# Two experts with small remainders share one block of rows

## The chip, the cores and the metric

The kernel runs on one core of a Trainium2 chip. The time is the device time of one launch in microseconds (us). The kernel before took 860.69 us in the median of three runs (860.58 to 861.32). A core has five engines with instruction queues of their own: TensorE (PE: products, into the PSUM memory), VectorE (DVE), ScalarE (ACT), GpSimd (POOL) and SyncE (SP, here a queue for transfers). Each works through its own queue in order and waits on semaphores for the others. Transfers run on 16 DMA engines; a transfer belongs to the queue of the engine that issues it.

## The reference

Two decoder layers, each of attention, cross-attention and a feed-forward part, run over x of 4 x 256 tokens with 256 features. All parts but the last are the same in both kernels. The last one is a mixture of experts: each token chooses 6 of 28 experts, and their outputs are summed with the softmax weights of the choice.

```python
logits = x @ gate_weight.T
scores = softmax(logits)
topk_w, topk_idx = top_k(scores, 6)
topk_w = topk_w / (topk_w.sum(-1) + 1e-20)
cw = zeros((T, E)).at[arange(T)[:, None], topk_idx].add(topk_w)
for wg, wu, wd, w_tok in zip(w_gate, w_up, w_down, cw.T):   # 28 experts
    h = silu(x @ wg) * (x @ wu)                               # 256 -> 176
    y = y + w_tok[:, None] * (h @ wd)                         # 176 -> 256
```

Here T is 1024, so there are 6144 pairs of a token and an expert. On the reference's inputs an expert gets between 117 and 302 tokens.

## The kernel before

**Lists and blocks.** `_route` writes, for each of the four batches, every token's row (its 256 features, its number as an integer, the weights of all its experts; 288 values) into DRAM, once for each chosen expert: into `lists`, where every expert has room for 1024 rows. `lists` is filled beforehand with blank rows, whose numbers point to spare rows behind the result (1024 to 1151). The work is then cut into *blocks*: 128 rows of one expert. When an expert's number of tokens is not a multiple of 128, its last block is filled up with blank rows.

Twelve blocks (`EARLY`) that are full after five of the eight token tiles start early, while the last batch is still being routed. `_blocks` counts the tokens of each expert, subtracts the early blocks, takes the running sum over experts by a product with a triangular matrix, and `_tables` makes three tables of NBLK entries from it: the expert of each block (packed in words for TensorE's registers), the row of `lists` at which it starts (for SP's registers), and the expert's number on every partition. The code runs `USUAL` = 50 late blocks without a condition, and the rest, up to NBLK, under `tc.If`. On these inputs there are 50 late blocks.

**One block.** `load` fetches 128 rows (xb; the pool has EARLY + 2 = 14 buffers). `turned` transposes them on TensorE (tpx) and copies them out on ScalarE (Tx). `gate_up` multiplies by the expert's gate and up weights, which lie in SBUF for all experts at once and are addressed by a register (pgu, 352 columns, two steps over the features), then SiLU on ScalarE (sg) and a product on VectorE (eh). `hidden` transposes eh and copies it out on VectorE (Th). `down` multiplies by the down weights (py, two steps of 88), picks the row's weight for this expert on VectorE (wjunk, wsel), scales on ScalarE (ys; NACC + 2 = 5 buffers), and GpSimd adds the 128 rows into an accumulator in DRAM by an indirect transfer, at the token numbers that xb carries (L998). A float32 product appears in the trace as two matmul records, so a block has four for pgu and four for py.

**The order.** In `rest`, step j issues the load of block j + 4, then gate_up(j), down(j - 1), turned(j + 2) and hidden(j). A scheduler then sets each engine's final order. In `early`, down is put off by LAG = 8 steps, because the down weights arrive late.

**The accumulators.** There are NACC + NLATE = 5 arrays. Their adds go round in turn; two adds into the same array wait for each other. From block LATE = 16 on, only the last two arrays are used, and in the meantime the other three are read back and added to x: `sums` loads a pair of token tiles (part; 6 buffers), and VectorE adds them (L1085), spread over the steps by `join_sums`. When all blocks are done, the last two arrays are read back in eight loads on the queues of SP and ACT (L1072), added (L1103), and the output is written (L1104).

Of the kernel before, what the change touches and what calls it, by code (L numbers as in the profile page):

```python
# [11 lines left out]
F32 = mybir.dt.float32  # L12
I32 = mybir.dt.int32
BF16 = mybir.dt.bfloat16
AF = mybir.ActivationFunctionType
ALU = mybir.AluOpType
# [4 lines left out]
P = 128  # L21
B, S, C = 4, 256, 256
# [11 lines left out]
E, M, TOPK = 28, 176, 6  # L34
MH = M // 2
# [1 line left out]

EARLY, FULL = 12, 5
SURE = min(EARLY, (FULL * P * TOPK - E * (P - 1) + P - 1) // P)
NBLK = (B * S * TOPK + E * (P - 1)) // P - SURE  # L40
TRASH = E * B * S
ROW = 288
NACC = 3
USUAL = 50
NLATE, LATE = 2, USUAL - 34


K_ID, K_MASK, K_TRI, K_ONES = 0, 128, 256, 384
# [2 lines left out]
K_BLK = K_BASE + E  # L51
K_STEP = K_BLK + NBLK
K_OF = K_STEP + B * S // P
# [823 lines left out]
def _blocks(nc, tc, env):  # L877

    psum, cst, ones, tri, rt1, seen, done = (env[n] for n in ("psum", "cst", "ones", "tri", "rt1", "seen", "done"))
    pn = psum.tile([P, 8], F32, tag="tp", name="pn")  # L880
    nc.tensor.matmul(pn[:E, 0:1], seen[:, NT], ones[:, 0:1], start=True, stop=True)
    cnt = rt1.tile([E, 1], F32, name="cnt")
    nc.vector.tensor_copy(cnt, pn[:E, 0:1])
    nb = rt1.tile([E, 1], F32, name="nb")
    junk = rt1.tile([E, B * S // P], F32, name="bjunk")
    nc.vector.tensor_scalar(junk, cst[:E, K_STEP:K_OF], cnt, None, ALU.is_lt, ALU.add, accum_out=nb)
    nc.vector.tensor_tensor(nb, nb, done, ALU.subtract)
    yield
    pc = psum.tile([P, 8], F32, tag="tp", name="pcum")
    nc.tensor.matmul(pc[:E, 0:1], tri[:E, :E], nb, start=True, stop=True)  # L890
    nc.tensor.matmul(pc[:E, 1:2], ones[:E, :E], nb, start=True, stop=True)
    first = rt1.tile([E, 2], F32, name="first")
    nc.vector.tensor_copy(first, pc[:E, 0:2])
    total = rt1.tile([1, 1], I32, name="total")
    nc.vector.tensor_copy(total, first[0:1, 1:2])
    off = rt1.tile([E, 1], F32, name="off")
    nc.vector.tensor_tensor(off, cst[:E, K_OF : K_OF + 1], done, ALU.add)
    nc.vector.tensor_tensor(off, off, first[:, 0:1], ALU.subtract)
    env["rest"], _ = yield from _tables(nc, env, "1", NBLK, first[:, 0:1], nb, off)
    env["total"] = total  # L900


class _Blocks:


    AHEAD = 4
    LAG = 8

    def __init__(self, ctx, nc, tc, env):
        self.nc, self.tc, self.psum, self.cst, self.ident = (nc, tc, env["psum"], env["cst"], env["ident"])  # L910
# [4 lines left out]
    def begin(self, ctx, wdn):  # L915
        self.wdn = wdn
        self.ek = ctx.enter_context(self.tc.tile_pool(name="ek", bufs=2))

    def values(self, table, engine, top, j, n):
        _, vals = self.nc.values_load_multi_w_load_instructions(  # L920
            table[:, j : j + n],
            [engine],
            min_val=0,
            max_val=top,
            skip_runtime_bounds_check_because="the table's entries are clamped to these bounds",
        )
        return vals

    def words(self, table, n):

        nc = self.nc
        loaded = self.values(table, mybir.EngineType.PE, (1 << 20) - 1, 0, (n + 3) // 4)

        def expert(i):
            e = nc.tensor.snap((loaded[i // 4] >> (5 * (i % 4))) & 31)
            return nc.s_assert_within(
                e, 0, E - 1, skip_runtime_bounds_check_because="the table's entries are clamped to these bounds"
            )

        return expert  # L940

    def load(self, row, queue):
        xb = self.eb.tile([P, ROW], F32, tag="xb", name="xb")
        queue.dma_start(xb, self.lists[bass.ds(row, P), :])
        return xb
# [9 lines left out]
    def gate_up(self, xT, e):  # L955
        nc = self.nc
        g = self.psum.tile([P, 2, 512], F32, tag="sc", name="pgu")
        pg = g[:, 0, : 2 * M]
        for k in range(2):
            nc.tensor.matmul(  # L960
                pg, xT[:, k, :], self.wgu[:, bass.ds(e * (4 * M) + k * 2 * M, 2 * M)], start=(k == 0), stop=(k == 1)
            )
        sg = self.ek.tile([P, M], F32, tag="sg", name="sg")
        nc.scalar.activation(sg, pg[:, :M], AF.Silu)  # L964
        h = self.ek.tile([P, M], F32, tag="h", name="eh")
        nc.vector.tensor_tensor(h, pg[:, M:], sg, ALU.mult)  # L966
        return h, g[:MH, 1, : 2 * P].rearrange("p (k n) -> p k n", k=2)

    def hidden(self, h, tp):
        for k in range(2):  # L970
            self.nc.tensor.transpose(tp[:, k, :], h[:, k * MH : (k + 1) * MH], self.ident)  # L971
        hT = self.ek.tile([MH, 2, P], F32, tag="Th", name="Th", bufs=self.LAG + 2)
        self.nc.vector.tensor_copy(hT, tp)  # L973
        return hT

    def down(self, hT, e, xb, e_col, accs):
        nc = self.nc
        wsel = self.ek.tile([P, 1], F32, tag="wsel", name="wsel")
        junk = self.ek.tile([P, E], F32, tag="wjunk", name="wjunk")
        done = nc.vector.scalar_tensor_tensor(  # L980
            junk,
            self.cst[:, K_IOTA : K_IOTA + E],
            e_col,
            xb[:, C + 1 : C + 1 + E],
            ALU.is_equal,
            ALU.mult,
            accum_out=wsel,
        )
        if not self.puts:
            _stay_behind(self.tc, done, self.route["placed"])  # L990
        py = self.psum.tile([P, C], F32, tag="o", name="py")
        for k in range(2):
            nc.tensor.matmul(  # L993
                py, hT[:, k, :], self.wdn[:, bass.ds(e * (2 * C) + k * C, C)], start=(k == 0), stop=(k == 1)
            )
        y = self.ek.tile([P, C], F32, tag="ys", name="ys", bufs=NACC + 2)
        nc.scalar.activation(y, py, AF.Copy, scale=wsel)  # L997
        nc.gpsimd.indirect_dma_start(  # L998
            out=accs[self.puts % len(accs)],
            out_offset=bass.IndirectOffsetOnAxis(ap=xb[:, C : C + 1].bitcast(I32), axis=0),  # L1000
            in_=y,
            in_offset=None,
            compute_op=ALU.add,
        )
        self.puts += 1

    def load_early(self, rows):
        at = self.values(rows, mybir.EngineType.Pool, TRASH, 0, EARLY)
# [2 lines left out]
    def early(self, engine, words, rows, e_all):  # L1011
# [3 lines left out]
        es, hTs, before = [], [], None  # L1015
        for j in range(EARLY + self.LAG):
            if j < EARLY:
# [5 lines left out]
            if j + 2 < EARLY:  # L1023
                xTs.append(self.turned(xbs[j + 2]))
            if j >= self.LAG:
                n = j - self.LAG
                self.down(hTs[n], es[n], xbs[n], e_all[:, n : n + 1], self.acc)
            yield

    def rest(self, words, list_row, e_all):  # L1030
        nc = self.nc
        expert = self.words(words, NBLK)
        at, xbs = {}, {}

        def load(j, end):
            if j not in at:
                n = min(5, end - j)
                at.update(zip(range(j, j + n), self.values(list_row, mybir.EngineType.SP, TRASH, j, n)))
            xbs[j] = self.load(at.pop(j), nc.sync)

        def run(first, end, also=None):
            for j in range(first, min(first + self.AHEAD, end)):
                load(j, end)
            xTs = {j: self.turned(xbs[j]) for j in range(first, first + 2)}
            before = None
            for j in range(first, end):
                if j + self.AHEAD < end:
                    load(j + self.AHEAD, end)
                e = expert(j)
                h = self.gate_up(xTs.pop(j), e)  # L1050
                if before is not None:
                    self.down(*before)
                if j + 2 < end:
                    xTs[j + 2] = self.turned(xbs[j + 2])
                accs = self.acc if j < LATE else self.acc[NACC:]
                before = (self.hidden(*h), e, xbs.pop(j), e_all[:, j : j + 1], accs)
                if also is not None:
                    also(j)
            self.down(*before)

        return run


def _experts(ctx, nc, tc, x, out, env):

    acc = env["acc"]
    ep = ctx.enter_context(tc.tile_pool(name="ep", bufs=6))


    def sums(n, q, queue):  # L1070
# [7 lines left out]
    def join_sums(j):  # L1078
# [4 lines left out]
        if 0 <= j - LATE - 10 < len(adds):  # L1083
            n, t = adds[j - LATE - 10]
            nc.vector.tensor_tensor(x[t], x[t], parts[n, t // 2][:, t % 2, :], ALU.add)  # L1085

    run = env["blocks"].rest(*env["rest"])
    more = nc.values_load(
        env["total"], min_val=0, max_val=NBLK, skip_runtime_bounds_check_because="a sum of rounded counts, at most NBLK"
    )  # L1090
    run(0, USUAL, join_sums)
    with tc.If(more > USUAL):
        run(USUAL, NBLK)

    oview = out.rearrange("b (t p) c -> (b t) p c", p=P)
    queues = (nc.sync, nc.scalar)
    for q in range(NT // 2):
        late = [sums(NACC + n, q, queues[n]) for n in range(NLATE)]
        for i in range(2):
            t = 2 * q + i  # L1100
            engine = nc.gpsimd if t % 3 == 2 else nc.vector
# [791 lines left out]
def _constants():  # L1893
# [8 lines left out]
    c[:, K_BASE:K_BLK] = np.arange(E) * B * S + 1  # L1902
    c[:, K_BLK:K_STEP] = np.arange(NBLK)
    c[:, K_STEP:K_OF] = np.arange(B * S // P) * P
# [107 lines left out]
```

## Time and profile before

| | us |
|---|---|
| median of three runs | 860.69 |
| the profiled execution | 860.22 |
| its span, first to last instruction | 858.6 |
| first product of the late blocks | 702.3 |
| end of the last product | 839.9 |
| tail, last product to the end of the span | 18.7 |
| TensorE busy, 702.3 to 840.0 | 131.9 of 137.7 |
| VectorE, ScalarE, GpSimd busy in the same stretch | 54.1, 52.0, 81.9 |
| mean granted TensorE clock, whole span | 0.883 of full speed |

A line of the timeline gives the start, the length, the engine, the line of the kernel, the operation with output and inputs, and in brackets the idle time of the engine just before and what ended it. A line of the chain gives start, length, engine, tile and line; a step of the chain is cut where the next one begins. A line of the groups by form gives, after the count, the busy time in us and the mean of one in ns, then idle time before them. A line of the waits gives who waited for whom, the total in us, how often, and the longest. Ends of matmuls are modelled, so the distance from start to start is the better measure of them.

### The profile page before, as it was taken

The numbers are of one execution on the slowest core, as the hardware profiler recorded it, in microseconds if no ns is written. First come the engines' busy times: TensorE is split into PE (matmuls) and PEld (weight loads), VectorE is DVE, ScalarE is ACT, GpSimd is POOL, SyncE is SP. The second block draws the span as 40 slices with busy tenths as digits, with TensorE's granted clock in tenths as the row PEclk, the third lists the DMA queues.
The fourth block names the chain that finished last, engine by engine and source line by source line (L and its number), as shares of the span: only waits on it lengthen the run. The fifth ranks groups of instructions, "written<-read, shape, count | busy, mean of one in ns | idle before, by whom it ended". The sixth has DMA issues, their size and how long they took to land. (4 is left out here: it accounts for less than half of the span.)

```text
span 858.6 us, 12259 instructions
## 1 busy us (share of the span) xinstructions
PE 700.7 (82%) x3902; PEld 458.1 (53%) x3902; DVE 526.0 (61%) x1306; ACT 304.7 (35%) x992; POOL 324.6 (38%) x280
## 2 busy tenths in 40 slices
PE   8988998588988887979568646897888789889991
PEld 4546555355555564566325325565545457667770
DVE  4677567886563699885538996756545223353332
ACT  2255444342441401221046424455323134334430
POOL 3332122214220373430144530124455376546563
PEclk9999999789999796988788876999768699989996
DMA  8999999500505200141500000571137577767646
GB/s 302 281 337 324 326 326 331 204 1 0 185 19 214 77 2 0 46 151 50 165 1 1 0 1 1 213 300 63 63 114 200 188 128 119 149 173 112 104 56 167
DMA packets 84452, 117.94 MB, mean 137 GB/s; under 512 B 5822, under 2 KB 71487, under 8 KB 83874
## 3 DMA queue, kind: packets, MB, share of 16 engines
q1 hardware_dynamic: 70914, 98.56, 35.0%
q0 software_dynamic: 11808, 16.98, 11.2%
q10 hardware_dynamic: 1664, 1.57, 0.5%
q8 instruction: 35, 0.57, 0.3%
q14 instruction: 31, 0.25, 0.1%
HBM read 59.67 MB, written 55.33 MB: 134 GB/s over the span
## 5 line engine op out<-in xcount | busy, mean ns | idle before, releaser
L998 POOL DMA_INDIRECT acc<-ys,xb x62 | 97.7, 1576 | 71.2 <-ACT Tx L952 43.4
L960 PE MATMUL pgu<-wgu_e,Tx 128*128 x248 | 93.7, 504 | 5.5 <-ACT Tx L952 3.3
L417 POOL TENSOR_TENSOR pr<-pr,rs 128x512 f32<-128x512 f32 x32 | 41.9, 1312 | 131.8 <-DVE rs L415 69.1
L407 ACT ACTIVATE pr<-sc,nb 128x256 f32<-128x256 f32 x128 | 58.9, 474 | 49.8 <-DVE nb L402 49.6
L993 PE MATMUL py<-wdn_e,Th 88*128 x248 | 65.4, 391 | 4.7 <-DVE Th L973 2.8
L1749 ACT ACTIVATE xpr<-xsc,cnm 128x256 f32<-128x256 f32 (+1 forms) x128 | 52.1, 421 | 39.7 <-DVE cnm L1744 28.4
L797 POOL DMA_INDIRECT lists<-R,rows x48 | 47.0, 979 | 37.4 <-DVE rows L784 13.6
L960 PEld LDWEIGHTS pgu<-wgu_e,Tx 128*128 128x128 f32 x248 | 46.0, 205 | 24.5 <-issue 7.1
L993 PEld LDWEIGHTS py<-wdn_e,Th 88*128 88x128 f32 x248 | 47.4, 195 | 21.2 <-DVE Th L973 3.9
L1557 POOL TENSOR_TENSOR qk<-qkv 128x1024 f32<-128x1024 f32 x16 | 39.9, 2524 | 35.8 <-ACT qkv L1528 35.8
L107 PE MATMUL av<-pT,ckt 128*64 128x256 f32 x256 | 39.8, 409 | 15.4 <-DVE pT L433 10.5
L966 DVE TENSOR_TENSOR eh<-pgu,sg 128x176 f32<-128x176 f32 x62 | 21.0, 339 | 48.3 <-issue 26.0
L964 ACT ACTIVATE sg<-pgu 128x176 f32<-128x176 f32 x62 | 19.7, 317 | 76.3 <-PE pgu L960 64.5
L997 ACT ACTIVATE ys<-py,wsel 128x256 f32<-128x256 f32 x62 | 29.3, 473 | 44.5 <-PE py L993 35.8
L107 PE MATMUL xsc<-kz,xqT 64*128 64x128 f32 (+1 forms) x256 | 37.7, 397 | 7.5 <-ACT xpr L1749 6.5
L110 PE MATMUL x_tp<-cst,xpr 128*128 128x128 f32 x192 | 34.3, 309 | 10.4 <-ACT xrT L1792 3.3
L398 DVE TENSOR_REDUCE nm<-sc 128x4 f32<-128x1024 f32 x32 | 39.0, 1217 | 4.9 <-PE sc L107 4.5
L980 DVE SCALAR_TENSOR_TENSOR wjunk<-cst,e_all,xb 128x28 f32<-128x28 f32 x62 | 15.3, 247 | 42.7 <-ACT ys L997 41.9
L1549 POOL TENSOR_TENSOR qk<-qkv 128x1024 f32<-128x1024 f32 x16 | 35.6, 2254 | 14.2 <-ACT qkv L1521 8.6
L1611 DVE TENSOR_TENSOR pv<-s,qkv 128x2048 f32<-128x2048 f32 x16 | 40.6, 2538 | 0.1
L110 PE MATMUL tp<-cst,pr 128*128 128x128 f32 x256 | 38.1, 291 | 2.4 <-DVE pT L433 1.5
L1576 PE MATMUL as<-qk,cst 128*128 128x128 f32 x256 | 34.6, 298 | 6.1 <-POOL qk L1549 6.1
(377 smaller groups left out, 1569.7 us busy)
## 6 DMA issues: line engine op xcount, KB each, us to landing
lists<-blank SPq DMA_DIRECT2D x9, 3600.0 KB
wgu_e<-in_e_gu_dram SPq DMA_DIRECT2D x4, 2464.0 KB
xb<-lists SPq DMA_DIRECT2D x50, 144.0 KB
acc<-blank SPq DMA_DIRECT2D x5, 1152.0 KB
wdn_e<-in_e_dn_dram SPq DMA_DIRECT2D x4, 1232.0 KB
wq<-in_m_wq_dram SPq DMA_DIRECT2D x4, 1024.0 KB
mwo<-in_m_wo_dram SPq DMA_DIRECT2D x2, 2048.0 KB
part<-acc SPq DMA_DIRECT2D x16, 256.0 KB
```

The costliest lines, as they stand in the source:

```text
L107: self._next(self.engine.matmul(*args, **kw))
L110: self._next(self.engine.transpose(*args, **kw))
L398: nc.vector.tensor_reduce(nm, sc, AX.X, ALU.max, negate=True)
L407: nc.scalar.activation(pr[:, e, qt, :], sc[:, e, qt, :], AF.Exp, bias=nb[:, e, qt : qt + 1], accum_out=ss[:, e, qt : qt + 1],)
L417: nc.gpsimd.tensor_tensor(pr[:, 1], pr[:, 1], rs[:, 1].unsqueeze(2).to_broadcast([P, 2, S]), ALU.mult)
L797: done = nc.gpsimd.indirect_dma_start(out=lists, out_offset=bass.IndirectOffsetOnAxis(ap=rows[:, i, n : n + 1], axis=0), in_=R[:, i, :], i ...
L960: nc.tensor.matmul(pg, xT[:, k, :], self.wgu[:, bass.ds(e * (4 * M) + k * 2 * M, 2 * M)], start=(k == 0), stop=(k == 1))
L993: nc.tensor.matmul(py, hT[:, k, :], self.wdn[:, bass.ds(e * (2 * C) + k * C, C)], start=(k == 0), stop=(k == 1))
L998: nc.gpsimd.indirect_dma_start(out=accs[self.puts % len(accs)], out_offset=bass.IndirectOffsetOnAxis(ap=xb[:, C : C + 1].bitcast(I32), axi ...
L1557: nc.gpsimd.tensor_tensor(pr[:, 4 * i : 4 * i + 4], q3[:, h0 : h0 + 4].unsqueeze(2).to_broadcast([P, 4, H, D]), k3.unsqueeze(1).to_broadca ...
L1611: nc.vector.tensor_tensor(pv, s[:, hh].unsqueeze(2).to_broadcast([P, 8, D, H]), v3.unsqueeze(1).to_broadcast([P, 8, D, H]), ALU.mult,)
L1749: nc.scalar.activation(pr[:, j, cols], sc[:, j, cols], AF.Exp, bias=nm[:, i, j : j + 1], accum_out=ss[:, i, h : h + 1])
```

## The change

An expert's remainder of at most 64 tokens no longer gets a block of its own. `_blocks` now counts two kinds: blocks that are full or have more than 64 tokens, and small remainders. Both get tables, by two calls of `_tables`. Two small remainders share one block, each in one half of the rows: a *pair*.

- For a pair, `copied` copies the gate, up and down weights of both experts on ScalarE from where they lie (addressed by a register on ScalarE) to fixed tiles gu and dn, one buffer each.
- `halves` gives, for a pair, the products of either half of the rows: 64 rows of the block against that half's copied weights, into the 64 partitions of that half in PSUM. So pgu and py have twice as many products in a pair, each with half the output rows.
- The load of a pair is two transfers of 64 rows.
- `down` sends a pair's y out twice, so that tokens which chose both experts are not added twice in one transfer: once with the first half at its token numbers and the second half at spare rows (`aside`), once the other way round, into two accumulators in turn. Four small copies on VectorE (both) make the two columns of numbers.
- `rest` now runs 37 blocks (`USUAL`) and 7 pairs (`UPAIR`), mixed so that every sixth item is a pair. More of either kind runs under `tc.If`.
- LATE becomes 37 + 7 - 34 = 10, counted in items. LAG becomes 5 for 8, and the pool of `part` has 3 buffers for 6.

```diff
-USUAL = 50
-NLATE, LATE = 2, USUAL - 34
+USUAL, UPAIR = 37, 7
+NLATE, LATE = 2, USUAL + UPAIR - 34
...
+    big = rt1.tile([E, 1], F32, name="big")
+    nc.vector.tensor_scalar(junk, cst[:E, K_STEP:K_OF], cnt, None, ALU.is_lt, ALU.add, accum_out=big)
+    nc.vector.tensor_tensor(nb[:, 0:1], big, done, ALU.subtract)
+    nc.vector.tensor_tensor(nb[:, 1:2], every, big, ALU.subtract)
...
+    bigs, _ = yield from _tables(nc, env, "1", NBLK, first[:, 0:1], nb[:, 0:1], off[:, 0:1])
+    (words, rows, e_all), _ = yield from _tables(nc, env, "2", E, first[:, 1:2], nb[:, 1:2], off[:, 1:2])
...
-    LAG = 8
+    LAG = 5
...
+    def halves(self, e):
+        if not isinstance(e, tuple):
...
+        return [
+            (
+                slice(i * HALF, (i + 1) * HALF),
+                lambda k, i=i: e[0][:, i, k * 2 * M : (k + 1) * 2 * M],
+                lambda k, i=i: e[1][:, i, k * C : (k + 1) * C],
+            )
+            for i in range(2)
+        ]
+    def copied(self, experts):
+        nc = self.nc
+        gu = self.ew.tile([P, 2, 4 * M], F32, tag="gu2", name="gu2")
+        dn = self.ew.tile([MH, 2, 2 * C], F32, tag="dn2", name="dn2")
+        for i, e in enumerate(experts):
+            nc.scalar.copy(gu[:, i], self.wgu[:, bass.ds(e * (4 * M), 4 * M)])
+            nc.scalar.copy(dn[:, i], self.wdn[:, bass.ds(e * (2 * C), 2 * C)])
+        return gu, dn
...
         for k in range(2):
-            nc.tensor.matmul(
-                pg, xT[:, k, :], self.wgu[:, bass.ds(e * (4 * M) + k * 2 * M, 2 * M)], start=(k == 0), stop=(k == 1)
-            )
+            for rows, gu, _ in self.halves(e):
+                nc.tensor.matmul(pg[rows], xT[:, k, rows], gu(k), start=(k == 0), stop=(k == 1))
...
         for k in range(2):
-            nc.tensor.matmul(
-                py, hT[:, k, :], self.wdn[:, bass.ds(e * (2 * C) + k * C, C)], start=(k == 0), stop=(k == 1)
-            )
+            for rows, _, dn in self.halves(e):
+                nc.tensor.matmul(py[rows], hT[:, k, rows], dn(k), start=(k == 0), stop=(k == 1))
...
+        places = [xb[:, C : C + 1].bitcast(I32)]
+        if isinstance(e, tuple):
+            both = self.ek.tile([P, 2], I32, tag="both", name="both")
+            for i in range(2):
+                for n in range(2):
+                    half = slice(n * HALF, (n + 1) * HALF)
+                    nc.vector.tensor_copy(both[half, i : i + 1], (places[0] if i == n else self.aside)[half])
+            places = [both[:, i : i + 1] for i in range(2)]
+        for place in places:
+            nc.gpsimd.indirect_dma_start(
+                out=accs[self.puts % len(accs)],
+                out_offset=bass.IndirectOffsetOnAxis(ap=place, axis=0),
...
+            self.puts += 1
...
+            for i in range(2):
+                nc.sync.dma_start(
+                    xb[i * HALF : (i + 1) * HALF], self.lists[bass.ds(row(kind, 2 * j + i, 2 * end), HALF), :]
+                )
+            copies[j] = self.copied([experts[1](2 * j + i) for i in range(2)])
...
+            items = [(0, j, b) for j in range(a, b)]
+            for j in range(c, d):
+                items.insert((j - c + 1) * ((b - a) // (d - c) + 1) - 1, (1, j, d))
...
-    ep = ctx.enter_context(tc.tile_pool(name="ep", bufs=6))
+    ep = ctx.enter_context(tc.tile_pool(name="ep", bufs=3))
...
-    run(0, USUAL, join_sums)
-    with tc.If(more > USUAL):
-        run(USUAL, NBLK)
+    run(((0, USUAL), (0, UPAIR)), join_sums)
+    with tc.If(more > 0):
+        run(((USUAL, NBLK), (UPAIR, E // 2)))
```

## The prediction

> **What bounds the kernel now.** I read the chain of waits first. From 702.3 us to 839.9 us the kernel runs its 50 late expert blocks, and the chain there stays on TensorE:
>
> ```profile
> 805.64 1.22 PE pgu L960 x4
> 806.86 0.86 PE py L993 x4
> 807.73 0.22 PE tpx L950 x2
> 807.95 0.22 PE pgu L971 x2
> 808.16 1.22 PE pgu L960 x4
> ```
>
> One block is four steps of TensorE, and the next starts 808.16 - 805.64 = 2.52 us later; over other blocks the mean is 2.53. 50 x 2.53 = 126.5 of the stage's 137.6 us; the rest is filling and a stall of 9 us near 746 to 766 us, where VectorE's adds of partial sums (L1085) wait for their loads and block the copies queued behind them (the waits, from 700 us to the end):
>
> ```profile
> DVE x_in L1103 <- DMA part<-acc: 11.2, 2, 9.8
> DVE x_in L1085 <- DMA part<-acc: 7.4, 4, 3.3
> ```
>
> Then ScalarE in the timeline, one step (start, length):
>
> ```profile
> 709.57 0.32 ACT L964 ACTIVATE sg<-pgu 128x176 f32<-128x176 f32 x1 [0.91 <-PE pgu L960]
> 710.44 0.47 ACT L997 ACTIVATE ys<-py,wsel 128x256 f32<-128x256 f32 x1 [0.55 <-PE py L993]
> 710.81 0.36 ACT L952 COPY Tx<-tpx 128x256 f32<-128x256 f32 x1
> 712.13 0.32 ACT L964 ACTIVATE sg<-pgu 128x176 f32<-128x176 f32 x1 [0.96 <-PE pgu L960]
> ```
>
> It has gaps of 0.55 and 0.96 us in each step: the room for anything put on ScalarE. Last, the adds into DRAM. From LATE on only two accumulators take them, so each waits for the one two before it. SP's block loads wait for the same completions (it loads 14 blocks ahead, into buffers that these adds free), so their times tell when an add is done:
>
> ```profile
> 798.44 1.56 POOL L998 DMA_INDIRECT acc<-ys,xb  x1 [0.97 <-ACT Tx L952]
> ...
> 803.79 1.56 POOL L998 DMA_INDIRECT acc<-ys,xb  x1 [1.27 <-ACT Tx L952]
> ...
> 809.53 1.56 POOL L998 DMA_INDIRECT acc<-ys,xb  x1 [2.00 <-DMA acc<-ys,xb]
> ```
>
> ```profile
> 803.26 0.33 SPq L944 DMA_DIRECT2D xb<-lists  x1
> 809.00 0.33 SPq L944 DMA_DIRECT2D xb<-lists  x1
> ```
>
> The add of 798.44 frees its buffer at 803.26 (4.8 us), that of 803.79 at 809.00 (5.2), and GpSimd starts the next one 0.53 later. These two are the slowest; the sixteen from 768 to 806 us take 3.9 to 5.2, mean 4.2.
>
> **The change part by part.** *Blocks.* Routing the reference's own inputs gives 50 late blocks before; after, 37 blocks of one expert and 13 remainders of at most 64 tokens, so 7 pairs. This fills USUAL and UPAIR exactly and the conditional part stays out. 44 items for 50: 6 x 2.53 = -15.2 us.
>
> *Half-row products.* A pair issues twice the products, each with 64 output rows. The nearest row is the first attention's av (128 contracted, 64 columns, two halves in turn, 256 moving), on TensorE's timeline:
>
> ```profile
> 201.99 1.08 PE L107 MATMUL av<-pT,ckt 128*64 128x256 f32 x8
> 203.00 0.48 PE L107 MATMUL po<-Bp,aT 128*128 128x256 f32 x1
> ```
>
> Eight take 1.01 us to the next start, where py's four full ones take 0.86 and eight in series would take 1.72: the halves overlap, but for one step of the stagger (5 units for 4). So py +0.2; pgu, 352 wide, a quarter of 1.22 = +0.3; 0.5 a pair, 7 x 0.5 = +3.5. Against the change speaks the Trainium skill, TensorEngine Tiling, Key Properties: a change of the tiling mode, more than of the tile, drains TensorE. A pair changes mode four times. The row bounds a drain by how long a product outlasts the next one's start (201.99 + 1.08 - 203.00 = 0.07; for py 1.03 - 0.86 = 0.17): 4 x 0.17 x 7 = 4.8 on top of the stagger would make +8.3. I take +3.5, since av stands between products of other modes and its 1.01 holds a switch. No overlap at all: 7 x 2.08 = +14.6.
>
> *Weight copies on ScalarE.* Four a pair: two of 128x704, two of 88x512. Nearest rows, by form:
>
> ```profile
> L431 ACT COPY pT<-tp 128x512 f32<-128x512 f32 x32 | 18.8, 589 | 46.1 <-PE tp L110 46.0
> L1707 ACT COPY kz<-xpk 128x1024 f32<-128x1024 f32 x4 | 4.0, 1014 | 0.6 <-PE xpk L1706 0.6
> L1786 ACT COPY xwide<-crs 128x256 f32<-128x256 f32 x8 | 3.3, 412 | 2.5 <-DVE crs L1784 1.5 <-DVE ln_mv L169 1.0
> ```
>
> (1014 - 589)/512 = 0.83 ns an element; a source in SBUF adds some 0.04 us (412 for xwide, 365 for Tx): 0.79 and 0.63, 2.84 a pair. The built order splits them: the two large stand after one step's sg, ahead of its ys and Tx; the small after the next step's Tx, ahead of the next sg. Behind the large: 1.58 + the register work of the expert's number against gaps of 0.55 + 0.96 = 1.51, so the next sg is some 0.15 late. The small: 1.26 against 0.96, sg 0.3 late plus registers; eh, hidden's products and TensorE behind it follow at once, as eh ends 0.1 before TensorE wants it. I take 0.5 a pair for six (the first pair's copies come before the stage): +3. Ends: 0, and all 2.84 exposed, +17.
>
> *Two scatters a pair.* One y goes out twice, the other half's rows aside to spare rows. GpSimd: 51 for 50 at 1.86, not its limit. The accumulators are. From item 16 on: 28 items and 5 pairs, TensorE 28 x 2.53 + 5 x 1.0 = 75.8; 33 adds, 32 intervals of (4.2 + 0.53)/2 = 2.37: 75.8 too. Two limits that meet cost for their scatter: +1, ends 0 and +9 (spacing 5.3). When adds fall behind, the five ys fill, ys waits on ScalarE, and Tx and sg behind it hold TensorE. The skill (DMA: Bandwidth & Descriptors, Rules for kernel authors) says why the wait can't be dropped: an accumulate loses what is written between its read and its write. The price is the trace's.
>
> *Partial sums with 3 buffers for 6.* Before, loads 0 to 5 go out before any add; now load 3 waits for the adds of load 0, 6 for 3's, 9 for 6's. On SP they also stand between block loads, which wait for adds into DRAM delayed by the same stall. One more wait of about a landing (3.35 us in the chain at 745.36) less the step it lies in: 9 us becomes 11, +2 (0 to +6). A stall near 3 us also leaves products at half pace (py 2.08 for 0.86 at 749.65).
>
> *Tail.* Before, seven of eight loads go out at once at 845.5 and the last lands at 852.1. Three buffers make three rounds of landing (some 2.5), adds (1.5) and reissue, with output writes between the loads on SP and ACT: some 15 us for 13.2, +2 (0 to +4).
>
> *Start of the stage.* LAG 5 for 8 lets four products and ys run at once when the down weights land (681.0). The early adds started at 683.84, 687.01, 689.28, 691.55, and then every 1.86; all at 1.86 from the first, the seventh starts at 695.0, not 697.13. It frees ys for the twelfth, behind which stand the late stage's first Tx: -2. Against it: the second table (17 small VectorE operations near 0.17, 3 us) and ScalarE's wait for its words with the first 2.84 us of copies stand ahead of the first ys. VectorE and ScalarE both wait until 675 there, which puts the words near 679 and ys near 683, as before (683.1). Ends -2.5 and +3.
>
> *Covered.* Four copies of 64x1 a pair on VectorE (near 0.14, as cnt): its 0.9 us before eh; uncovered 0.6 a pair, +4. Split loads on SP: 14 blocks ahead; uncovered 0.4 each, +3.
>
> Sum: -15.2 + 3.5 + 3 + 1 + 2 + 2 - 2 = -5.7. From the profiled execution's 860.2 (span 858.6): 854.5. The median of the runs, 860.69, is 0.5 above that execution: 855.0.
>
> **The rivals.** *The two accumulators bound the stage* (slower). Place: adds from item 16. Price: 32/2 x the spacing above 4.73. It takes the 5.7 and my 1 from 4.73 + 6.7/16 = 5.15 us on; at 5.3, +9.1 for +1: 863. For: both quoted spacings (5.35, 5.74), and three adds in flight where two were. Against: the mean of 4.7, and early adds at 1.86 apart that were done in 3.9 to 4.5.
> *Half-row products run in series*: +14.6 for 3.5, 866. Against: av.
> *The copies are twice as dear*: 3.2 and 2.5 us against 1.5 and 0.96, 3.2 a pair, 19 for 3: 871. For: no SBUF copy of this width in the trace. Against: the even slope of three rows.
> *Three buffers cost both their upper ends*: +6 and +4 for 2 and 2: 861.
>
> **How the numbers follow.** Forecast 0.62 (own range 851 to 859), accumulators 0.16, buffers 0.12, series 0.04, copies 0.04, the rest 0.02. The range leaves about 0.1 on each side: 849.5 (copies and sums at their lower ends) to 863. No change, within 0.2% (1.7 us, about what this kernel's measurement can tell), takes half of the buffers' case and a little of the accumulators': 0.08. Slower 0.20, faster 0.72.
>
> **What would show it.** Pair rows for pgu and py with eight products in near 1.5 and 1.05 us; gu and dn copies near 0.79 and 0.63; sg late by under 0.6 after them; first late pgu near 700; late adds waiting for "DMA acc" now and then, ys rarely; the last add done near 838. Wrong if ys waits for DMA in most pair steps, if py's eight take 1.7, or if the time from the last add to the end exceeds 17 us.

## The result, and the profile after

The changed kernel took 884.86 us in the median (880.52 to 890.14), the kernel before on the same chip 861.01: a ratio of 1.0269, 95% interval 1.0205 to 1.0333. Forecast were 855.0 us and "faster"; it is 2.7% slower, and outside the range. The profiled execution took 880.52 us, with a span of 878.9; it was the fastest of four, so the stretches below add up to 20.3 us more than before, and not to the 23.9 of the medians.

Where the time went shows in four stretches, each cut at the same events in the two traces:

| stretch (us) | before | after | forecast of the difference |
| --- | --- | --- | --- |
| first ys of the early blocks to first late gate-and-up product | 19.2 | 20.4 | -2 |
| first late product to last product | 137.6 | 144.8 | -5.7 |
| last product to last add into DRAM | 5.5 | 9.5 | 0 (its +1 is in the row above) |
| last add to the end | 13.1 | 16.6 | +2 |

Another 4.5 us lie ahead of the first row: the first early ys is at 687.6 for 683.1.

The chain of waits of the changed kernel is no longer on TensorE from end to end. One cycle of five single blocks and a pair reads (start, length; "issue" is time for which the profile shows nothing that was waited for):

```profile
766.38 1.33 PE pgu L1022 x8
767.72 1.06 PE py L1054 x4
...
769.22 1.19 PE pgu L1022 x4
770.40 1.04 PE py L1054 x8
...
771.47 0.48 ACT ys L1056
771.95 0.27 issue
772.22 3.76 DMA acc<-ys,both
775.97 2.47 issue
778.44 0.15 DVE both L1064
...
779.12 0.35 DVE eh L1026
779.48 0.04 issue
779.52 0.42 PE pgu L1031 x2
779.94 2.14 PE pgu L1022 x4
782.08 1.71 PE py L1054 x4
...
786.74 1.33 PE pgu L1022 x8
```

The pair's own products are as cheap as hoped: eight of pgu in 1.33 us, eight of py in 1.04. But after the pair's y has gone out at 772.22, the chain goes from GpSimd's DMA to VectorE's tiny copies `both` (L1064), through eh, and back to TensorE, which then runs the next block at nearly half pace (pgu 2.14 for 1.19, py 1.71 for 0.86). The granted clock shows it: 1.00 up to 780 us, then 0.65, 0.50, 0.50 and 0.64 in four steps of 1 us, and 1.00 from 784 on. From one pair to the next it takes 786.74 - 766.38 = 20.36 us, where six blocks of 2.53 are 15.2.

VectorE's timeline at the same place (start, length, and in brackets the idle time before and what ended it):

```profile
774.77 0.42 DVE L1033 COPY Th<-pgu 88x256 f32<-88x256 f32 x1
778.44 0.15 DVE L1064 COPY both<-xb 64x1 int32<-64x1 int32 x1 [3.25 <-issue]
778.60 0.31 DVE L1064 COPY both<-aside 64x1 int32<-64x1 int32 x2
778.94 0.15 DVE L1064 COPY both<-xb 64x1 int32<-64x1 int32 x1
779.12 0.34 DVE L1026 TENSOR_TENSOR eh<-pgu,sg 128x176 f32<-128x176 f32 x1
```

These four copies belong to the pair that comes twelve items after the one whose y has just gone out, nine after the block in hand. VectorE takes its queue in order, so eh of the block in hand stands behind them, and TensorE behind eh. The waits from 700 us to the end (sum, times, longest) in the changed kernel, and then the one for eh in the kernel before:

```profile
PEld pgu L1031 <- DVE eh L1026: 18.5, 10, 3.2
...
DVE both L1064 <- issue: 13.0, 4, 3.5
...
DVE both L1064 <- DMA xb<-lists: 5.4, 3, 2.0
```

```profile
PEld pgu L971 <- DVE eh L966: 4.3, 4, 3.3
```

TensorE's weight loads (PEld) waited 4.3 us for eh before, and 18.5 now. The `both` copies wait 18.4 us in all, in seven waits. Their busy time, which is what the prediction priced, is 0.15 us each.

In the changed kernel's program the first `both` copy of a pair waits for two things: the landing of its own block, and the two scatters that read the same buffer of `both` for the pair two before (the pool has two buffers). GpSimd's timeline shows the second at work:

```profile
772.22 1.55 POOL L1067 DMA_INDIRECT acc<-ys,both  x1 [0.56 <-ACT ys L1056]
774.57 1.55 POOL L1067 DMA_INDIRECT acc<-ys,both  x1 [0.81 <-DVE eh L1026]
```

The second scatter of the pair in hand starts at 774.57, and the copy runs 3.87 us later. An add into DRAM took 3.9 to 5.2 us in the kernel before, so the copy starts about when the scatter can have landed.

### The profile page after: what moved, and what is told of

Same layout as the page of the kernel before. It is cut to its first block, busy times and chain, and to the rows that moved or that the text cites. A ratio compares the mean times of both kernels' runs of the same rounds, so it can differ in the third digit from the quotient of the medians.

```text
span 878.9 us, 12187 instructions
## 1 busy us (share of the span) xinstructions
PE 696.4 (79%) x3890; PEld 447.1 (51%) x3890; DVE 525.7 (60%) x1332; ACT 314.6 (36%) x1002; POOL 328.2 (37%) x283
## 5 line engine op out<-in xcount | busy, mean ns | idle before, releaser
L1067 POOL DMA_INDIRECT acc<-ys,xb x49 | 78.7, 1606 | 70.1 <-ACT Tx L1013 41.9
L1022 PE MATMUL pgu<-wgu_e,Tx 128*128 x196 | 77.6, 524 | 5.0 <-DVE Th L1033 2.0
L1054 PE MATMUL py<-wdn_e,Th 88*128 x196 | 56.4, 419 | 9.5 <-DVE Th L1033 5.1
L1054 PEld LDWEIGHTS py<-wdn_e,Th 88*128 88x128 f32 x196 | 39.9, 211 | 27.0 <-DVE Th L1033 9.0
L1022 PEld LDWEIGHTS pgu<-wgu_e,Tx 128*128 128x128 f32 x196 | 37.6, 211 | 20.9 <-issue 7.5
L1026 DVE TENSOR_TENSOR eh<-pgu,sg 128x176 f32<-128x176 f32 x56 | 19.0, 339 | 47.5 <-ACT sg L1024 42.7
L1024 ACT ACTIVATE sg<-pgu 128x176 f32<-128x176 f32 x56 | 17.8, 318 | 78.3 <-PE pgu L1022 55.1
L1056 ACT ACTIVATE ys<-py,wsel 128x256 f32<-128x256 f32 x56 | 26.4, 473 | 41.3 <-PE py L1054 38.3
L109 PE MATMUL sc<-ckv,qk 64*128 64x256 f32 x256 | 39.2, 408 | 0.8 <-ACT qk L386 0.8
L1031 PE MATMUL pgu<-cst,eh 128*88 128x128 f32 x112 | 23.0, 289 | 20.0 <-DVE eh L1026 19.9
## 6 DMA issues: line engine op xcount, KB each, us to landing
xb<-lists SPq DMA_DIRECT2D x37, 144.0 KB
```

The source lines that it names most:

```text
L109: self._next(self.engine.matmul(*args, **kw))
L1022: nc.tensor.matmul(pg[rows], xT[:, k, rows], gu(k), start=(k == 0), stop=(k == 1))
L1054: nc.tensor.matmul(py[rows], hT[:, k, rows], dn(k), start=(k == 0), stop=(k == 1))
L1067: nc.gpsimd.indirect_dma_start(out=accs[self.puts % len(accs)], out_offset=bass.IndirectOffsetOnAxis(ap=place, axis=0), in_=y, in_offset=None,
```

## The experiments

The runs were made on several chips, on which the kernel before had medians from 845.06 to 862.5 us; each ratio is to the kernel before on the same chip, with its 95% interval in brackets, and microseconds "of 861" are that ratio times 861.

**The copies behind their own pair's work, the start, and both.** Both copies of indices and ScalarE's first work for the pairs are put behind an instruction that is on the same engine anyway, so only the order in the queues changes.

```
# e1_both_late, in down(): done is the pair's own wjunk
-                    nc.vector.tensor_copy(both[half, i : i + 1], ...)
+                    one = nc.vector.tensor_copy(both[half, i : i + 1], ...)
+                    _stay_behind(self.tc, one, done)
# e2_start: the words' load and the first weight copies behind the last early ys
+            for one in self.reg_loads:
+                _stay_behind(self.tc, one, self.last_ys)
...
-            nc.scalar.copy(gu[:, i], ...)
+            one = nc.scalar.copy(gu[:, i], ...)
+            _stay_behind(self.tc, one, self.early_ys)
# e3_both_start: e1 and e2 together
```

> The changed kernel with one thing moved: the four copies into 'both' of a pair must follow that pair's own wjunk on VectorE; before, the scheduler had put them some two pairs ahead, where they wait for a block load that waits for an add into DRAM, with eh and Th queued behind them. Theory 1 (these early copies hold VectorE's queue): in the changed kernel the items of a pair's cycle take 20.4 us for six (pgu-eh from 779.5 to 799.95 to 820.6) where 16 were forecast; with the copies late, about 16 to 16.5, and so some 4.5 us for each of five or six cycles: time 884.9 falls by 20 to 27 us, to 858 to 865. Theory 2 (the two accumulators bound the late stage, the waits of the copies only show it): the cycles stay near 20, the time falls by less than 4 us, and ys or the adds take over the waiting.

> The changed kernel with another thing moved: ScalarE's load of the pairs' register words and the first pair's weight copies must follow the last early ys. Theory 1s (they delay the start of the late stage, since all early ys stand behind them and the words come from the second table): the first early ys comes back from 687.6 to about 683 us, the first late pgu from 708.0 to 701 to 704, time falls by 4 to 7 us. Theory 2s (the start is late for another reason: the product of the early blocks or VectorE's early copies into 'both'): first ys moves, but the first late pgu stays within 2 us of 708, time falls by less than 2.

> Both moves of the two runs before together. If both theories 1 and 1s hold they should add: 25 to 33 us below 884.9, so 852 to 860, near the forecast of 855. If the two are one cause (VectorE's early copies also hold the early blocks) it is no better than the first alone by more than 2 us.

Measured: e1 1.0034 (1.0018 to 1.0050), so 20 us of 861 less than the changed kernel's 1.0269. e2 1.0222 (1.0185 to 1.0260), 4 us less, though the two intervals overlap. e3 0.9989 (0.9961 to 1.0016), 24 us less, and 4 less than e1: the two add up as far as can be told, and what is left cannot be told from the kernel before. In e3 TensorE's timeline has one pair after the other at

```profile
783.07 1.40 PE L1026 MATMUL pgu<-gu,Tx 128*64 128x352 f32 x8
...
787.09 1.08 PE L1058 MATMUL py<-dn,Th 88*64 88x256 f32 x8
...
798.73 1.40 PE L1026 MATMUL pgu<-gu,Tx 128*64 128x352 f32 x8
```

798.73 - 783.07 = 15.66 us for 20.36, at a granted clock of 1.00 throughout. The pair therefore costs 15.66 - 6 x 2.53 = 0.48 us, its weight copies included. The place of the copies in the queue is the cause of the loss. e1 does not tell which of the two waits it was, since it took both away.

**The start.** ScalarE's timeline of the changed kernel, and then of e2, where the early ys begin:

```profile
685.16 1.46 ACT L999 COPY gu<-wgu_e 128x704 f32 x2 [3.49 <-issue]
686.52 1.13 ACT L1000 COPY dn<-wdn_e 88x512 f32 x2
687.56 0.82 ACT L1056 ACTIVATE ys<-py,wsel 128x256 f32<-128x256 f32 x2
```

```profile
683.12 0.47 ACT L1060 ACTIVATE ys<-py,wsel 128x256 f32<-128x256 f32 x1 [1.57 <-PE py L1058]
683.99 0.47 ACT L1060 ACTIVATE ys<-py,wsel 128x256 f32<-128x256 f32 x1 [0.39 <-PE py L1058]
```

The weight copies, which wait for the pairs' words, began at 685.2 where the words had been estimated near 679, and they stood ahead of the early ys. In e2 alone the first ys came 4.4 us earlier, but the first late product no earlier (707.8 for 708.0), against the 701 to 704 that were expected: the `both` copies of the first pairs then held VectorE just there (ys stop from 692.4 to 700.1). In e3 the stretch from the first ys to the first late product is 16.9 us for 19.2 before. That looks like the -2 of the LAG step, so LAG was changed alone:

```
# b_lag5: the kernel before
-    LAG = 8
+    LAG = 5
```

> The kernel before with LAG 5 for 8 and nothing else: the early blocks' down products and their ys can follow the down weights' landing in a bunch. The prediction put this at -2 us (-2.5 to 0): ratio 0.9977. Rival 'the ys and Tx queue on ScalarE takes it back': ratio within 0.002 of 1, with the first late gate-and-up product no earlier after the first early ys than 19 us.

Measured 0.9988 (0.9966 to 1.0009), and 19.1 us from the first ys to the first late product: the stretch is no shorter, and the interval holds a gain of 2 us as well as none. In f1, m1 and f5 below, whose start is e3's, it is 18.9, 19.5 and 17.7 us. The 16.9 of e3 are one execution; a gain from LAG was not shown.

**Three buffers for the partial sums.**

```
# b_bufs3: the kernel before
-    ep = ctx.enter_context(tc.tile_pool(name="ep", bufs=6))
+    ep = ctx.enter_context(tc.tile_pool(name="ep", bufs=3))
```

> The kernel before with the pool of part cut from 6 to 3 buffers, nothing else. My terms: +2 for the partial sums in the middle of the stage and +2 for the tail, so 861.0 becomes 865, between 861 and 871. The changed kernel's tail (last add landed to the end) is 16.6 us for 13.2: if that is the buffers, this run's tail is 16 to 17 too, +3.4 us; if it is the pairs, 13.2.

Measured 1.0050 (1.0026 to 1.0073), 4.3 us of 861. In its trace the stage grows from 137.6 to 139.4 us and the tail from 13.1 to 17.0, both from this one edit. The tail's chain shows the three rounds:

```profile
845.70 2.95 DMA part<-acc
...
850.25 3.65 DMA part<-acc
...
854.96 3.71 DMA part<-acc
```

Before, one landing stood there:

```profile
846.57 5.52 DMA part<-acc
```

**One scatter for each pair.** It prices the second add. The rows of the pair's second expert are added nowhere.

```
# m1_one_scatter: e3, and
-        for place in places:
+        for place in places[:1]:
```

> The kernel of e3_both_start with one scatter for each pair instead of two: the rows of the pair's second expert are not added anywhere, everything else stays. It prices the second scatter by itself. Theory 'the doubled scatters queue at the two accumulators and are paid at the end': e3 had 14.5 us from the last product to the last add, the kernel before 5.5; without the seven extra adds the 14.5 falls to about 6, and the time from 859 to about 850. Rival 'the long drain has another cause (the loads of partial sums, the later block loads)': the drain stays near 14 us and the time within 1 us of 859.

**More buffers for the tail, and pairs closer together.** f1 gives the memory of the weight copies back after the last block and takes five more buffers for the last loads; f2 puts a pair after every three single blocks; f3 does both.

```
# f1_tail: e3, and
+    held = ExitStack()
-    env["blocks"].begin_rest(ctx)
+    env["blocks"].begin_rest(held)
...
+    held.close()
+    more_parts = ctx.enter_context(tc.tile_pool(name="ep2", bufs=5))
# the last loads: ep for the first three, more_parts for the others
# f2_every4: e3, and
-                items.insert((j - c + 1) * ((b - a) // (d - c) + 1) - 1, (1, j, d))
+                items.insert((j - c + 1) * 4 - 1, (1, j, d))
```

> e3_both_start with the tail's part buffers given back: the memory of the weight copies is released after the last block and five more buffers for the last eight loads of partial sums are taken from it, so that all eight loads can go out at once. Theory 'three buffers cost the tail 4 us': last add to end falls from 17.3 to about 13, the time from 859 to about 855. Rival 'the tail is long for another reason': 17 us and 859 stay.

> e3_both_start with a pair after every three single blocks instead of every five, so that the last pair is item 28 of 44 and not 42. Two pairs instead of one fall before LATE, where five accumulators take the adds. Theory 'the two accumulators are short of capacity, whatever the place': one add fewer in the late part is 2.4 us, and 16 single items at 2.53 against a spacing of about 2.37 win back 2.5: drain 10 to 12 us, time about 855. Rival 'the drain is only the last two pairs' bunching': drain 6, time 850. Rival 'a denser row of pairs is not hidden on ScalarE and at the ys buffers': the stage grows by 3 or more, time 861 or above.

> f1_tail and f2_every4 together. If the tail and the drain are separate costs, their gains add: about 851, 1.1% below the kernel before. If the earlier pairs only shift the wait, 855 as f1_tail.

These four ran on one chip, with the kernel before at 845.06. m1 has a ratio of 0.9836 (0.9797 to 0.9876), f1 0.9952 (0.9934 to 0.9969), f2 1.0043 (1.0027 to 1.0059), f3 1.0011 (0.9994 to 1.0029).

The chain of m1, and then that of f1, at the end of the adds. In m1 TensorE's last py starts at 807.61, in f1 at 809.73:

```profile
799.67 15.00 DMA acc<-ys,xb
814.66 0.03 ACTq L1170
```

```profile
805.63 19.42 DMA acc<-ys,xb
825.05 0.02 SPq L1170
```

From the start of the last py to the last add it is 7.1 us in m1 and 15.3 in f1; the stretch from the first early ys to the last py is 141.3 and 144.0. The second scatter costs 8.2 us in the drain, as the time from the last product to the last add is called here, and 2.7 on the way: about 11, where the forecast had 1. Against e3, which differs from m1 by this edit alone but ran on another chip, the ratios give 13, 4 more or less, where 9 were expected. After the last product m1's drain is 6 us, as expected. Most of the price is paid after the last product and little in the stage, which fits a TensorE that runs on, through the five ys buffers, while the adds fall behind. It also fits that the drain is longer in e1 and e3 (14.0 and 14.5 us after the last product) than in the changed kernel (9.5): a faster stage gives part of its gain back there.

f1 did most of what it should: the tail is 14.5 us for e3's 17.3, where about 13 were expected. f2 did not: the drain, from the start of the last py, is 12.4 for e3's 15.7, but the stretch to the last py is 153.6 for f1's 144.0. The rival with denser pairs holds. The first late product comes 4 us later (688.57 for 684.60); a round of three single blocks and a pair takes 10.9 us, which makes the pair 0.8 dearer than a single block where e3 has 0.48; the rest is in the part where the sums are joined. Why a denser row of pairs loses that much was not taken apart. The gain of f1 and the loss of f2 add up in f3: from e3's 0.9989 they make 1.0006, and 1.0011 was measured.

**A later LATE.** Ten more items use all five accumulators.

```
# f5_late20: f1, and
-NLATE, LATE = 2, USUAL + UPAIR - 34
+NLATE, LATE = 2, 20
# join_sums: two adds a step for one, three steps after their load
```

> f1_tail with LATE at 20 for 10: ten more items add into all five accumulators, and the sums of the three early ones are joined two tiles a step for one, so that they still end before the last item. Of the pairs four for six fall to the two late accumulators: 28 adds at 2.37 us are 66.4 us against 24 x 2.53 + 4 x 0.47 = 62.6 of TensorE's, where f1 has 40 x 2.37 = 94.8 against 88.8. Theory 'the two accumulators are short of capacity from LATE on': the drain after the last product falls from 15.3 to about 12 us, and the ratio to the kernel before from 0.9952 to about 0.991. Rival 'the joining of the sums is dearer two a step': the stall there grows by more than 4 us and the ratio is 0.996 or above.

Measured 0.9909 (0.9883 to 0.9935), as expected. The drain, again from the start of the last py, is 11.3 us (828.79 to 840.04), 4 less than in f1. This version is 0.9% faster than the kernel before.

**Which of the two waits it was.** The first run frees the buffers of `both`, the second does so with the copies held at the very place in VectorE's queue that they have in the changed kernel.

```
# h_both7: the changed kernel, and
-            both = self.ek.tile([P, 2], I32, tag="both", name="both")
+            both = self.ek.tile([P, 2], I32, tag="both", name="both", bufs=7)
# h_same_place: h_both7, and (dones: the wjunk of every item)
+                    one = nc.vector.tensor_copy(both[half, i : i + 1], ...)
+                    if len(self.dones) > 9 and len(self.pairs_at) > 1:
+                        _stay_behind(self.tc, one, self.dones[self.pairs_at[-2] + 3])
```

> The changed kernel with seven buffers for the small tile 'both' instead of two, and nothing else; its four copies a pair still stand ahead of their turn on VectorE. In the built program of the changed kernel the first of these copies waits for two things: the landing of its own pair's block, and the two scatters of the pair that used the same of the two buffers before. e1_both_late, which moved the copies behind their own pair's work, took both waits away and cannot tell them apart; here only the second is gone. Theory 'the buffer: the copies wait for two scatters just issued' (the copy of 778.44 starts 3.87 us after the second scatter's start at 774.57): most of the 20.6 us of e1 come back, time 862 to 868 by the clock of the runs beside it, ratio about 1.004 to 1.009, and the waits of 'both' for 'issue' (13.0 us) vanish. Rival 'the block load: it waits for an add into DRAM that frees its buffer': the copies stand no later here, so they wait as long, ratio within 0.006 of 1.027.

> h_both7 freed the buffers, but its built program also put the copies one to two items earlier on VectorE, nearer to their block's load, and they waited for that load instead (19.7 us in nine waits). Here the seven buffers stay and the copies are held at the very place of the changed kernel: the order of every engine is the changed kernel's, and only the wait for the two scatters of the pair before is gone. Theory 'at that place the wait is the one for the scatters': the 13.0 us of waits by 'issue' vanish and the time falls by 13 to 20, ratio 1.004 to 1.012. Rival 'at that place the load is as late as the scatters': the copies wait for 'xb<-lists' in their stead, ratio 1.02 or above.

Measured: h_both7 1.0245 (1.0165 to 1.0326), where 1.004 to 1.009 were expected: no gain that can be told from the changed kernel's 1.0269; the interval is wide because the kernel before ran between 849 and 860 us beside it. h_same_place 1.0122 (1.0094 to 1.0149), 13 us of 861 less. The waits of h_both7 and then of h_same_place:

```profile
DVE both L1064 <- DMA xb<-lists: 19.7, 9, 5.6
```

```profile
DVE both L1066 <- DMA xb<-lists: 4.6, 3, 2.8
```

In both the waits by "issue" are gone. In h_same_place the pairs' pgu then follow one another as they do in e3, 833.05 - 817.40 = 15.65 us apart:

```profile
817.40 1.40 PE L1023 MATMUL pgu<-gu,Tx 128*64 128x352 f32 x8
...
833.05 1.40 PE L1023 MATMUL pgu<-gu,Tx 128*64 128x352 f32 x8
```

From the first pair's pgu to the last one's it is 106.4 us in h_same_place, 105.4 in e1 and 120.3 in the changed kernel. So at the place that the copies had, the wait of 13.0 us was the one for the scatters, and between the pairs it is nearly all of the loss. In h_both7 the scheduler moved the copies up by one to two items, nearer to their block's load, and there they waited for the load: one wait took the other's place.

What e1 gains beyond h_same_place, some 8 us, lies ahead of the first pair: from the first early ys to the first pair's pgu it is 38.7 us in h_same_place and 30.8 in e1. The longest wait of a `both` copy for its block's load (2.8 us) stands there. But the changed kernel, with copies at the same place, needs 35.5, so this part is not settled.

## Why the prediction was wrong

**Failed: the step "Covered".** It priced the four copies a pair at "its 0.9 us before eh; uncovered 0.6 a pair, +4", and the sum held nothing for them. It took the room that VectorE has in a step and the busy time of the copies. It asked neither where the built order puts them nor what they wait for. They stand nine items ahead of their pair and wait for scatters that GpSimd has just issued, and what is queued behind them is eh. Measured, the place of the copies costs 20 us (e1), five times the uncovered price, and 13 of them are the wait for the scatters (h_same_place). An estimate for the end of this step's range could have been had from the kernel before, a landing of an add for each pair: 7 x 3.9 = 27 us. The prediction named three signs of being wrong (ys waiting for transfers, py's eight at 1.7 us, a tail above 17 us). None of them came; it failed where it had named no sign.

**Blocks, half-row products and weight copies: right, and better than forecast.** 44 items for 50 came as said. Forecast for a pair were 0.5 for its products and about 0.4 for its copies; e3 shows 0.48 for both. The weight copies took what the rows gave, by form in the changed kernel:

```profile
L999 ACT COPY gu<-wgu_e 128x704 f32 x14 | 10.2, 776 | 3.5 <-issue 3.5
L1000 ACT COPY dn<-wdn_e 88x512 f32 x14 | 8.0, 618 | 0.0
```

0.78 and 0.62 us for 0.79 and 0.63, and the gaps on ScalarE hid them. pgu of a pair took 1.33, only 0.14 over a full one's 1.19 where 0.3 was forecast; the pair's py took 1.04, as av said. The full py right behind the pair's pgu took 1.06 for 0.86, which no term had named. The rule weighed against the row (the Trainium skill, TensorEngine Tiling (Array Packing), Key Properties: a change of the tiling mode drains TensorE) gives no price; the prediction's bound on it, from the trace, was 4.8 us for the seven pairs. All of a pair's extra time is 0.48 us, 3.4 for seven, copies and stagger included, so the row was the better guide and no drain of that size shows.

**Two scatters: right resource, wrong count and wrong place.** Forecast +1, measured about 11 (8.2 in the drain, 2.7 on the way). The step set 75.8 us of TensorE's against 75.8 of the adds' and called it a tie. But it counted from item 16, while LATE is USUAL + UPAIR - 34 = 10 after the change: 40 adds at 2.37 are 94.8 us, against 34 x 2.53 + 6 x 0.48 = 88.9 of TensorE's, 6 us short from the start. This count is an estimate; it leaves out the stall for the partial sums, in which both stand still for a while. The runs bear it out in order: by the same count m1 is not short, f5 is short by 3.8 us and f1 by 5.9, and their drains, from the start of the last py, are 7.1, 11.3 and 15.3. Nor was the delay to be looked for at ys and Tx: it shows after the last product. The rival "the two accumulators bound the stage" had the right resource, but it asked for a spacing of 5.15 us and more, where the plain number of adds was enough. The other rivals fell: the halves did not run in series, and the copies were not twice as dear.

**Partial sums and tail.** With b_bufs3 the stage grew by 1.8 us (forecast +2) and the tail by 3.9 (forecast +2, upper end +4): the right step, the tail at its upper end.

**Start of the stage.** The first weight copies, which wait for the words, began at 685 for 679, so their load and the first copies did delay the first ys, by 4.5 us; the prediction had named this and given +3 as the end. With both moves, e3 against e1, 4 us came back. The -2 of LAG was not shown.

Put together from what was measured, in us: the blocks -15.2, pairs 3.4, second scatter 11, buffers 5.7, start in e3 -2.3. That makes +2.6 for a kernel with the copies in their place; e3 was measured at -0.9, with an interval from -3.4 to +1.4. The terms are no better known than that: the buffers are 4.3 by the ratio of b_bufs3 for 5.7 in its trace, the scatter 11 to 13, and the start is one execution. Part of the difference lies ahead of the stage: in e3's profile the first early ys is 5.6 us earlier than in that of the kernel before. So even with the copies in their place the change could not be told from the kernel before; with f1's buffers it is 0.5% faster, and with f5's later LATE 0.9%.

## What to carry to other kernels

For every instruction that a change adds to an in-order queue, however short, look in the built order for where it stands and what it waits for; its price is that wait, each time that something on the path stands behind it, and not its busy time. A small tile that a transfer reads kept its buffer here until the transfer was done, so count its buffers against the time from issue to landing, and against how far ahead a scheduler may put its writer. Where adds go to few accumulators, set the number of adds from the real switch-over item on against TensorE's time from the same item, and look for the debt after the last product, not in the stage.

## What the runs showed of the hardware

Two sets of 64-row products side by side cost nearly nothing here: eight of pgu with 64 columns, 352 wide, ran in 1.33 us where four full ones took 1.19. Short gaps of TensorE cost twice. In the stall at 778 us TensorE stood still for 2.68 us:

```profile
779.52 0.42 PE L1031 MATMUL pgu<-cst,eh 128*88 128x128 f32 x2 [2.68 <-DVE eh L1026]
```

The next eight products then took 2.14 - 1.19 + 1.71 - 0.86 = 1.8 us more than usual, while the granted clock was down to 0.50. The gap and the slower products make 4.5 of the 4.7 us by which the cycle was longer. After the gaps that end at 735.91, 799.95 and 820.57 (2.33, 2.79 and 2.98 us) the granted clock went to 0.50 as well, each time within 1 us of the products' return and for 3 to 3.5 us, and then back to 1.00. In e3's cycle without a gap it stayed at 1.00.
